# Finding a row's sources by segments of 128 columns, and a new order of the opening with four lists made early

## The chip, the cores and the metric

One core of a Trainium2 chip. The metric is the time of one execution on the device, in microseconds; the median of several executions is quoted with the lowest and the highest. All runs below are of the state "fast" but one: a run of 1221.58 us of "sums at +8" is marked slow and left out of its ratio. A profile is of one execution. Two profiles of the same kernel can differ by 8 us in a stage (349.2 and 341.1 us for steps 20 to 110 of the changed kernel), so a difference of a few microseconds between single profiles proves little; single steps that no wait disturbs repeat within a few tenths.

Names: PE is TensorE (matmul), PEld its weight load, DVE is VectorE, ACT is ScalarE, POOL is GpSimd, SP is SyncE, which here only issues DMAs. "Gate n" is the start of the DVE add that opens step n of the main loop; there are 320 steps.

## The reference

One layer of a graph network, batch B = 16, N = 1024 nodes, D = 256, float32:

```python
pre_u = einsum('bud,dk->buk', h, W1[:d]);  pre_v = einsum('bvd,dk->bvk', h, W1[d:])
hidden = relu(pre_u[:, :, None, :] + pre_v[:, None, :, :] + b1)
S   = sigmoid(einsum('buvk,ko->buvo', hidden, W2)[..., 0] + b2[0])
a_t = einsum('buv,bud->bvd', S * adj, h)
m_t = einsum('uv,bud->bvd', adj, h) * h
out = beta1 * h + beta2 * (a_t @ Wa + ba) + beta3 * (m_t @ Wm + bm)
```

`adj` is sparse: a row has its diagonal and a handful of other entries. The kernel works only on the entries that are not zero.

## The kernel before

Each of eight blocks of 128 rows needs a **list**: for every row the columns of its entries (at most S = 24), which are then dealt out to slots. The main loop takes 128 slots a step: fetch the source's row from a table in HBM (POOL, indirect), fetch the adjacency value, expand the destination's part (PE), add, relu and weigh (DVE), sigmoid (ACT), and aggregate (PE). Three lists are made before the loop and five between its steps. A list is a Python generator; each `yield` ends a part, and `script` (opening) and `advance` (loop) say when the next part of which list is emitted.

```python
def small(name):                       # PSUM: this pool has two buffers
    return psm.tile([P, 512], FP, name="misc")
def aside(vt):                         # where a list's matmul results go
    return psc.tile([P, GD], FP, name="pc") if vt < EARLY else small("pl")
NF = 5; EARLY = 3                      # buffers of fetched rows; lists made early
def clear(i):
    nc.gpsimd.memset(fetched[i][:, N if 1 <= i <= EARLY else 0:], 0.0)

def lists(vt):
    key = fetched[vt + 1][:, :N] if vt < EARLY else big.tile([P, N], FP, name="key", bufs=1)
    nc.gpsimd.dma_start(key, adjT[vt * P:(vt + 1) * P, :])
    yield
    ...                                # key = (adj != 0) * (N - column)
    nc.scalar.activation(unread, key, AF.Sign, accum_out=count)      # ACT counts the entries
    for s in range(0, S, 8):
        yield
        nc.vector.max(top[:, s:s + 8], key)                          # the 8 largest of 1024 columns
        if s + 8 < S:                                                # mask them, in place
            nc.vector.scalar_tensor_tensor(key, key, top[:, s + 7:s + 8], key, ALU.is_lt, ALU.mult)
    ...
    yield
    pw = aside(vt)                     # "sums": four small matmuls, PE -> PSUM
    for i in range(4):
        nc.tensor.matmul(pw[:, i:i + 1], sums[:, i]..., R[:, 0:1], start=True, stop=True)
    yield
    nc.vector.tensor_scalar(from_, pw[:, 1:2], base, low_, ALU.add, ALU.max)   # "from": DVE reads them
    ...                                # slots, four small writes of `whose` by ACT, sources

def rows(k):                           # one row block of a table: two half products
    tab = big.tile([P, GD], FP, name="tab")        # pool of two buffers
    ...

for i in range(EARLY, NT):
    for o in (0, 4, 5, 6, 7, 8, 9, 11, 13, 15, 17)[i == EARLY:]:
        advance[20 * (i - EARLY) + o] = (i,)
loads = dict(zip((0, 1, 2, 6, 9, 13, 17, 23), turn[NT:]))   # hT loads, each with a copy of x into
                                                            # the second table, issued by ACT
```

`misc` matters later. The same two PSUM buffers take, among others, the transposes of a finished half (`LT`), a swap (`X`), the halves of the second table (`tab`) and the sums of every list after the early ones. `hT` is x transposed, loaded in pieces of 512 KB for PE's products. `whose` tells which destination a slot belongs to; ACT writes it by four small DMAs for each list.

## Time and profile before

| | |
|---|---|
| time, 3 runs | 1238.86 us (1235.62 to 1244.02) |
| opening, to gate 0 | 89.2 us |
| steps 0 to 20 | 81.5 us |
| steps 20 to 110 | 352.4 us |
| step 110 to the end | 705.4 us |
| one list on DVE | 14.4 us |

The stages come from the starts of the DVE add. Read each one for itself: the opening waits on chains between engines, the steps up to 110 carry the lists and DVE limits them, and afterwards PE and the DMA engines are near their limit. The lines of the profile are shown in the prediction.

### The profile page before, as it was taken

What the parts mean: (1) busy time and instruction counts of PE and PEld (TensorE: products, weight loads), DVE (VectorE), ACT (ScalarE), POOL (GpSimd) and SP (SyncE); (2) the same over time, 40 slices, a digit from 0 to 9 for tenths busy, and PEclk for the clock granted to TensorE, in tenths of its full rate; (3) what the DMA queues carried; (4) which work ended last, traced back from release to release, by engine and by line L of the source; (5) the groups of instructions that cost most, each with busy time, mean ns of one, the idle gap of its engine ahead of it and who ended that gap; (6) DMA issues with size and microseconds to landing.
All of it is one profiled execution on the core that took longest, in us unless ns stands there. A gap on an engine that the chain in (4) does not pass through costs nothing. (4 is left out here: it accounts for less than half of the span.)

```text
span 1228.5 us, 23863 instructions
## 1 busy us (share of the span) xinstructions
PE 1108.6 (90%) x7697; PEld 723.5 (59%) x7697; DVE 1094.8 (89%) x3437; ACT 841.1 (68%) x2562; POOL 425.5 (35%) x419
## 2 busy tenths in 40 slices
PE   4767998997979989999999999999999999999996
PEld 3654665654546555666666556666666555665553
DVE  7659888999999899999899999889888999999994
ACT  1236675775656757777777777777777777777763
POOL 2227362362623614422333323222222333333330
PEclk8768999999999989999999999999999999999998
DMA  9569898898898989999999999999999988999992
GB/s 295 181 245 360 282 349 305 284 334 284 259 331 297 327 291 343 350 358 361 348 362 368 337 347 318 345 345 405 386 354 335 345 320 315 325 339 326 325 334 95
DMA packets 151975, 393.50 MB, mean 320 GB/s; under 512 B 16816, under 2 KB 110512, under 8 KB 115632
## 3 DMA queue, kind: packets, MB, share of 16 engines
q0 software_dynamic: 49792, 300.90, 66.4%
q1 hardware_dynamic: 85488, 76.03, 19.3%
q10 hardware_dynamic: 16560, 14.95, 3.7%
q8 instruction: 63, 1.03, 0.3%
q14 instruction: 72, 0.59, 0.1%
HBM read 395.88 MB, written 50.33 MB: 363 GB/s over the span
## 5 line engine op out<-in xcount | busy, mean ns | idle before, releaser
L452 POOL DMA_INDIRECT fetched<-table,uidx x320 | 329.9, 1031 | 705.0 <-PE acc L561 493.6
L544 DVE SCALAR_TENSOR_TENSOR t<-t,w_b 128x256 f32<-128x256 f32 x1280 | 469.9, 422 | 19.3 <-ACT X L412 0.5
L540 DVE TENSOR_TENSOR t<-fetched,pc 128x1024 f32<-128x1024 f32 x320 | 389.0, 1216 | 50.3 <-PE pc L524 25.2
L561 PE MATMUL acc<-fetched,left 128*32 128x256 f32 x4096 | 323.7, 392 | 26.9 <-ACT left L550 25.7
L550 ACT ACTIVATE left<-left,gt 128x32 f32<-128x32 f32 (+1 forms) x1280 | 299.4, 304 | 10.4
L524 PE MATMUL pc<-X,mark 128*128 128x512 f32 x640 | 247.3, 468 | 3.4 <-DVE t L540 1.9
L561 PEld LDWEIGHTS acc<-fetched,left 128*32 128x32 f32 x4096 | 122.7, 109 | 193.4 <-issue 68.0
L547 ACT ACTIVATE gt<-sc,b_b 128x4 f32<-128x4 f32 x320 | 95.4, 298 | 190.0 <-DVE t L544 189.5
L378 PE MATMUL misc<-w_u,hT 128*128 128x256 f32 x512 | 131.6, 406 | 23.5 <-ACT tab L394 12.9
L609 PE MATMUL misc<-w_m,LT 128*128 128x256 f32 x496 | 133.7, 392 | 0.0
L524 PEld LDWEIGHTS pc<-X,mark 128*128 128x128 f32 x640 | 118.4, 193 | 25.1 <-DVE LT L592 4.1
L609 PE MATMUL misc<-w_a,LT 128*128 128x256 f32 x496 | 127.3, 379 | 0.0
L378 PEld LDWEIGHTS misc<-w_u,hT 128*128 128x128 f32 x512 | 99.3, 202 | 45.1 <-ACT tab L394 14.4
L378 PE MATMUL misc<-w_v,hT 128*128 128x256 f32 x512 | 123.0, 384 | 0.0
L534 ACT ACTIVATE left<-onehot,val 128x128 f32<-128x128 bf16 (+1 forms) x320 | 116.6, 364 | 0.0
L609 PEld LDWEIGHTS misc<-w_m,LT 128*128 128x128 f32 x496 | 88.9, 189 | 34.8 <-issue 25.5
L336 POOL DMA_INDIRECT val<-in_adjT_dram,vidx x80 | 84.0, 1050 | 66.8 <-DVE b_p L194 40.0
L378 PEld LDWEIGHTS misc<-w_v,hT 128*128 128x128 f32 x512 | 98.5, 192 | 13.4
L544 DVE DVE_READ_ACCUMULATOR t<-t,w_b 128x1 f32 x1280 | 104.0, 81 | 0.0
L609 PEld LDWEIGHTS misc<-w_a,LT 128*128 128x128 f32 x496 | 94.2, 190 | 12.8
L569 ACT COPY ev<-acc 128x512 f32<-128x512 f32 x128 | 74.8, 585 | 28.9 <-PE acc L561 28.9
L424 ACT CAST X<-misc 64x512 fp32r<-64x512 f32 x128 | 74.3, 581 | 28.0 <-PE misc L421 23.9
(138 smaller groups left out, 860.1 us busy)
## 6 DMA issues: line engine op xcount, KB each, us to landing
hT<-in_xT_dram SPq DMA_DIRECT2D x40, 512.0 KB, 11.1
table<-tab SPq DMA_DIRECT2D x32, 512.0 KB, 5.2
h_blk<-in_x_dram SPq DMA_DIRECT2D x31, 512.0 KB, 13.4
out_dram<-h_blk SPq DMA_DIRECT2D x31, 512.0 KB, 5.5
table<-in_x_dram ACTq DMA_DIRECT2D x24, 512.0 KB, 11.8
fetched<-table,uidx POOLq DMA_INDIRECT x320, 7.9
table<-in_x_dram SPq DMA_DIRECT2D x8, 512.0 KB, 8.0
key<-in_adjT_dram POOLq DMA_DIRECT2D x5, 512.0 KB, 9.2
```

The source lines that it names most:

```text
L336: nc.gpsimd.indirect_dma_start(out=val[:, i, j:j + 1], out_offset=None, in_=adj_flat, in_offset=bass.IndirectOffsetOnAxis(ap=vidx[:, i, j: ...
L378: nc.tensor.matmul(p[:, bb * D:(bb + 1) * D], hT[:, 2 * h + bb, i, :], wt[:, i, :], start=(i == 0 and not begun), stop=(i == DC - 1), skip ...
L452: nc.gpsimd.indirect_dma_start(out=fetched[n % NF], out_offset=None, in_=table[g], in_offset=bass.IndirectOffsetOnAxis(ap=uidx[:, vt * NW ...
L524: nc.tensor.matmul(pcs[n][:, c], marks[n // TW][:, j * P:(j + 1) * P], cuts[k][:, w, c], start=True, stop=True)
L534: nc.scalar.activation(lefts[n][:, :m, :, 0, :], onehot[:, i, o:o + m, :].unsqueeze(2).to_broadcast([P, m, GB, V]), AF.Copy, scale=val[:, ...
L540: nc.vector.tensor_tensor(t, fetched[n % NF][:, :GD].rearrange("p (b d) -> p b d", b=GB), pcs.pop(n).rearrange("p (b d) -> p b d", b=GB), ...
L544: nc.vector.scalar_tensor_tensor(t[:, b, :], t[:, b, :], 0.0, w2_b, ALU.max, ALU.mult, accum_out=sc[:, b:b + 1])
L547: nc.scalar.activation(gt, sc, AF.Sigmoid, bias=b2_b)
L550: nc.scalar.activation(lefts[n][:, :m, b, 1, :], lefts[n][:, :m, b, 0, :], AF.Copy, scale=gt[:, b:b + 1])
L561: nc.tensor.matmul(accs[h][b * 2 * V:(b + 1) * 2 * V, r, :], left[:, i, b].rearrange("p k v -> p (k v)"), f[:, GD + b * D:GD + (b + 1) * D ...
L569: nc.scalar.copy(evs[q], accs.pop(q))
L609: nc.tensor.matmul(pz[:, bb * D:(bb + 1) * D], LTs[k][:, c, 2 * h + bb, i, :], wt[:, c, :], start=False, stop=(i == 1 and c == DC - 1), sk ...
```

## The change

The intent is to find the sources of a row with one pass over the keys, not five, and to rearrange the opening so that nothing in it waits for a buffer. DVE takes the 8 largest keys of each of eight segments of 128 columns; what lies below the largest eighth key of any segment is cut off, and the three passes run over the 64 candidates. Keys aren't overwritten. The early keys and the first group's table rows sit in the buffers of fetched rows, the memsets go, and four lists are made early.

```diff
-        return psc.tile([P, GD], FP, name="pc") if vt < EARLY else small("pl")
+        return psc.tile([P, GD], FP, name="pc") if vt < EARLY - 1 else small("pl")
-    EARLY = 3
+    EARLY = 4
-    def clear(i):
-        nc.gpsimd.memset(fetched[i][:, N if 1 <= i <= EARLY else 0:], 0.0)
-        nc.gpsimd.dma_start(key, adjT[vt * P:(vt + 1) * P, :])
+        (nc.sync if 2 <= vt < EARLY else nc.gpsimd).dma_start(key, adjT[vt * P:(vt + 1) * P, :])
+        yield
+        for c in range(N // P):
+            nc.vector.max(cand[:, c, :], key[:, c * P:(c + 1) * P])
+        yield
+        nc.vector.tensor_reduce(cut, cand[:, :, 7], AX.X, ALU.max)
+        nc.vector.scalar_tensor_tensor(keys, keys, cut, keys, ALU.is_ge, ALU.mult)
         for s in range(0, S, 8):
-            yield
-            nc.vector.max(top[:, s:s + 8], key)
+            nc.vector.max(top[:, s:s + 8], keys)
             if s + 8 < S:
-                nc.vector.scalar_tensor_tensor(key, key, ...)
+                nc.vector.scalar_tensor_tensor(keys, keys, ...)
-        tab = big.tile([P, GD], FP, name="tab")
+        tab = big.tile([P, GD], FP, name="tab") if tab is None else tab
+    tabs = [fetched[0][:, :GD], *(f[:, GD:] for f in fetched)]
     ...                                   (a new `script` for the opening)
-    for i in range(EARLY, NT):
-        for o in (0, 4, 5, 6, 7, 8, 9, 11, 13, 15, 17)[i == EARLY:]:
-            advance[20 * (i - EARLY) + o] = (i,)
+    advance = {0: (3,), 2: (3,), 4: (3,)}
+    for i, n in zip(range(EARLY, NT), (0, 30, 50, 80)):
+        for o in (0, 4, 5, 6, 7, 9, 11, 13, 15, 17):
+            advance[n + o] = (*advance.get(n + o, ()), i)
```

Two details of this diff are easily passed over. In the last lines, 8 is gone from the offsets: the sums are emitted at step +7 and read at +9, where they were emitted at +8. And the cut with all three passes is one part, where the search had been spread over three.

More of the change, by code (lines that the diff above doesn't have):

```diff
@@ L250, in lists @@
         nc.scalar.activation(unread, key, AF.Sign, accum_out=count)
+        yield
+        cand = wk.tile([P, N // P, 8], FP, name="cand", bufs=2)
+        for c in range(N // P):
+            nc.vector.max(cand[:, c, :], key[:, c * P:(c + 1) * P])
+        yield
+        cut = wk.tile([P, 1], FP, name="cut", bufs=2)
+        nc.vector.tensor_reduce(cut, cand[:, :, 7], AX.X, ALU.max)
+        keys = cand.rearrange("p c e -> p (c e)")
+        nc.vector.scalar_tensor_tensor(keys, keys, cut, keys, ALU.is_ge, ALU.mult)
         for s in range(0, S, 8):
-            yield
-            nc.vector.max(top[:, s:s + 8], key)
+            nc.vector.max(top[:, s:s + 8], keys)
             if s + 8 < S:
-                nc.vector.scalar_tensor_tensor(key, key, top[:, s + 7:s + 8], key, ALU.is_lt, ALU.mult)
+                nc.vector.scalar_tensor_tensor(keys, keys, top[:, s + 7:s + 8], keys, ALU.is_lt, ALU.mult)
         used = wk.tile([P, S], FP, name="used", bufs=4)
@@ L383, in add_row, with rows @@
                          start=True, stop=False, skip_group_check=True)
-    def rows(k):
+    def rows(k, tab=None):
         g, nt = k
-        tab = big.tile([P, GD], FP, name="tab")
+        tab = big.tile([P, GD], FP, name="tab") if tab is None else tab
         for h in range(2):
@@ L460 @@
     turn += [(1, vt) for _, vt in turn]
-    for i in range(2):
-        next(made[i])
+    tabs = [fetched[0][:, :GD], *(f[:, GD:] for f in fetched)]
     for i in range(NT):
+        if i < 2:
+            next(made[i])
         load_hT(turn[i])
-    for i in range(NF):
-        clear(i)
-    for i in range(2, EARLY + 1):
-        next(made[i])
+        if i in (5, 7):
+            next(made[i // 2])
     COPIES = 2
@@ L471 @@
         copy_h(turn[i], nc.sync)
-    script = ("r r 0 0", "r r 0", "r r 0 1", "0 r 1", "0 0 r r", "0 r 1", "r 0 0 v 1 r", "1 r 2 2", "1 1 r r h",
-              "1 r h 2", "1 1 h 2", "2 f h h", "2 2", "2", "2 2")
+    script = ("r 0 0", "r r 0", "r 1", "0 r 1 1", "0 0 r r", "1 r 0 2 2", "r 0 0 v 2", "1 1 r r 2",
+              "r 1 r 3 3", "1 1 2 2 r h", "2 r r h 3", "2 2 3 h", "3 3 f h h")
     m = 0
@@ L483 @@
                 if m % 2 == 0:
-                    piece = rows(turn[m // 2])
+                    piece = rows(turn[m // 2], tabs[m // 2] if m // 2 < len(tabs) else None)
                     next(piece)
@@ L655, in tail @@
         after(step + 1, add)
-    advance = {}
-    for i in range(EARLY, NT):
-        for o in (0, 4, 5, 6, 7, 8, 9, 11, 13, 15, 17)[i == EARLY:]:
-            advance[20 * (i - EARLY) + o] = (i,)
+    advance = {0: (3,), 2: (3,), 4: (3,)}
+    for i, n in zip(range(EARLY, NT), (0, 30, 50, 80)):
+        for o in (0, 4, 5, 6, 7, 9, 11, 13, 15, 17):
+            advance[n + o] = (*advance.get(n + o, ()), i)
     loads = dict(zip((0, 1, 2, 6, 9, 13, 17, 23), turn[NT:]))
```

## The prediction

> **What bounds the kernel now.** The page first: PE is busy 1108.6 of 1228.5 us (90%), DVE 1094.8 (89%), and the three DMA queues together take 89.4% of the sixteen engines. No engine is alone at the top, so averages decide nothing; I ask stage by stage. From the starts of the 320 gates (the DVE add of L540, one per step) the trace of the kernel before has three stages.
>
> - Opening: the first gate starts at 89.2 us. Until then only tables and lists are made.
> - Steps 0 to 110: from 89.2 to 523.1 us, 3.94 us a step. The lists 3 to 7 are made here, between gates.
> - Steps 110 to 320: from gate 110 at 523.1 to gate 310 at 1179.1 us, 3.28 us a step. No lists. The change adds and removes nothing here.
>
> The opening, in the timeline of all engines (columns: start, us, engine, line, operation; in brackets the idle time before and who ended it):
>
> ```profile
> 2.57 6.26 POOL L238 MEMSET fetched<- 128x2048 f32 x5
> 3.50 5.69 DVE L116 TENSOR_SCALAR upto<-ukey 128x640 f32<-128x640 f32 x1
> 12.85 1.21 DVE L249 SCALAR_TENSOR_TENSOR fetched<-fetched,ukey 128x1024 f32<-128x1024 f32 x1
> 14.09 1.23 DVE L253 MAX8 R<-fetched 128x8 f32<-128x1024 f32 x1
> 15.45 1.28 DVE L255 SCALAR_TENSOR_TENSOR fetched<-fetched,R 128x1024 f32<-128x1024 f32 x1
> ...
> 34.21 1.07 ACT L394 COPY tab<-misc 128x512 f32<-128x512 f32 x2 [17.54 <-DMA table<-tab]
> ...
> 36.37 1.28 DVE L255 SCALAR_TENSOR_TENSOR fetched<-fetched,R 128x1024 f32<-128x1024 f32 x1 [13.04 <-ACT unread L250]
> ...
> 74.94 1.00 POOL L452 DMA_INDIRECT fetched<-table,uidx  x1 [11.79 <-issue]
> ...
> 89.16 1.21 DVE L540 TENSOR_TENSOR t<-fetched,pc 128x1024 f32<-128x1024 f32 x1
> ```
>
> Three things to see. The DVE's 640-column scalar operation, which takes 0.55 us in the lists, takes 5.69 us beside the POOL memsets. ACT stands 17.5 us because the two tab buffers are still being written out; behind it in ACT's order is the count of list 1, and because the search overwrites the keys that ACT counts, DVE stands another 13.0 us. So one shortage of buffers stops PE, ACT and DVE together. The fetches begin only at 74.9, when the last table write has landed.
>
> The windows say the same (per engine busy us and instructions, granted PE clock, DMA share, GB/s):
>
> ```profile
> 20.00:40.00 20.00, 6.20 (x20) 5.13 (x21) 6.68 (x20) 2.71 (x5) 0.00 (x0) 0.58 1.06 298
> 40.00:60.00 20.00, 17.28 (x79) 14.39 (x78) 14.02 (x41) 5.49 (x10) 8.04 (x8) 0.91 0.44 147
> 60.00:80.00 20.00, 11.44 (x46) 9.49 (x46) 10.88 (x34) 5.07 (x9) 6.52 (x7) 0.77 0.44 134
> ```
>
> DMA is full to 40 us and under half used from 40 to 80: the opening is then bound by the chain through DVE, PE and ACT, not by bandwidth.
>
> For the second stage, windows of 40 us:
>
> ```profile
> 280.00:320.00 40.00, 33.86 (x232) 21.29 (x229) 38.57 (x129) 24.34 (x75) 11.17 (x11) 0.96 0.71 240
> 600.00:640.00 40.00, 39.54 (x290) 26.09 (x290) 37.50 (x119) 31.51 (x97) 12.47 (x13) 1.00 0.99 366
> ```
>
> At 280 DVE is busy 38.6 of 40 us and DMA only 0.71; at 600 PE and DMA are at their limit. So the list steps are DVE-bound and later ones are not. A check: steps 20 to 110 take 523.1 - 170.7 = 352.4 us, at 3.28 us a step they would take 295. The excess of 57 us is 14.3 for each of four lists, which is what one list costs DVE (14.4, below): there the lists come through in full.
>
> **The Trainium skill.** "SBUF — State Buffer", Who interferes with whom: GpSimd and a DVE operation of the two-port kind (tensor_scalar among them) share a port pair that is locked for a whole instruction. The trace agrees: 5.69 against 0.55 us, ending 0.4 us after the memsets. "VectorE: DVE Perf Modes", The TRN2 errata: a Vector operation costs (N+151)/0.96 ns, so short ones are mostly fixed cost, and the page advises 512 elements or more. MAX8 on 1024 columns should take 1224 ns, the trace has 1.22 to 1.23 us; I use it for the short ones, which this trace doesn't have (290 ns for 128 columns, 224 for 64, as estimates). The same page, Two Vector instructions with no wait between them: the next may start before the last has ended. In the trace, short ones without a wait start some 0.08 us before that end. "TensorE: Matmul & The Clock Gate", What's actually happening: an idle PE gets half the clock; the trace has 0.58 granted at 20 to 40 us.
>
> **The change part by part.**
>
> 1. Search of a row. Before: three MAX8 (3 x 1.23) and two maskings (2 x 1.28) over 1024 columns, each waiting for the last: 14.09 to 20.61, 6.5 us with the first wait; 6.3 without it. After: eight MAX8 of 128 columns without waits, 8 x (0.29 - 0.08) = 1.7; a reduction, a cut, three MAX8 and two maskings over 64 columns, seven dependent ones at about 0.25 = 1.75. Sum 3.4, so 2.9 saved. The rest of a list is unchanged: keys 1.2, bookkeeping 0.25, slots 4.0 (37.57 to 41.61), sources 2.6 (46.63 to 49.27). A list falls from 14.4 to 11.5 us of DVE. The inputs give at most 7 sources in any segment, so nothing spills into the slow remainder.
>
> 2. The keys aren't overwritten any more, so the 13.0 us wait for ACT's count goes.
>
> 3. Memsets gone: 6.3 us of POOL, and DVE's setup ends some 5 us sooner (7.7 instead of 12.85). Key 0 lands at 9.95, so list 0 starts at about 10: 2.9 gained.
>
> 4. Eight tab buffers instead of two for the first group: the 17.5 us wait goes.
>
> 5. The fourth list (number 3) moves ahead of the first gate, all but its last 2.6 us. Steps 20 to 110 now hold three lists, not four; steps 0 to 20 hold list 4 and the remainder of list 3, 14.1 against 14.4 us.
>
> 6. Keys 2 and 3 move to the SP queue. The bytes moved before the first fetch are the same, some 14.7 MB; at the 300 GB/s of the opening they need 49 us. That's a floor above which the new opening still ends, see next.
>
> **The new opening by hand**, along the order of each engine in the built program. DVE: list 0 searched by 15, list 1 by 20, slots of list 0 by 24, key 2 by 27. ACT gives the list-0 result only after the issue of four small copies (3.1 us before, at 43.06), which in the built program wait for the landing of earlier transfers, of which eight may be open, in a full queue: 30 to 34. Then sources of 0, rest of list 2, slots of 1, key 3: 43 to 46. Same round trip for list 1: sources of 1 by 49 to 52, slots of list 2 by 53 to 56. In the after order PE makes the last table row (two half rows) behind list 2's matmuls; add 4 to 5 us for it, ACT's copies behind the next issue, and the last table write goes out at 59 to 63 and lands 3.5 us later (70.55 to 73.91 before). First fetch at 63 to 67, against 74.9: 8 to 12 us gained. The gate also needs list 3's slots on DVE (69 to 72), ACT's four copies and mark (3 us), PE's expansion (2 us): gate 0 at 73 to 76, against 89.2: 13 to 16 gained. After that the fetches compete with the second table's transfers (DMA share 1.03 in 80 to 120), so the start of the fetches counts as much as that of the gate: I take **11 us**.
>
> **Main part.** Steps 20 to 110: DVE work falls by 4 x 14.4 - 3 x 11.5 = 23 us. PE is at 88% there (246 of 280 us in 200 to 480), and 246/(280 - 23) would be 96%, just what it holds at 600, so nearly all of it can come through: I take **20 us**. Steps 0 to 20: nothing.
>
> Sum: 31 us. 1238.9 - 31 = **1208 us**.
>
> **Rivals.** (a) DMA is the bound through the first 200 us, and an earlier start only moves the queue: the shares of 0.90 to 1.03 speak for it; against it, DVE waits for fetched rows in only 17.6 us in all after 80 us. Then the opening gives 5 and the sum is 25: 1214. (b) PE takes over when DVE is lighter in steps 20 to 110, as clock dips to 0.92 to 0.96 there hint; then the main part gives 10 and the time is 1218. (c) Everything before the first gate comes through, with PE warmer: 16 + 23 = 39 us, 1200. (d) The new order makes a fresh wait: ACT holds table copies behind the slots of a list, SP holds writes behind that; if list 2 comes 10 us later than I think, the opening gives nothing and the time is 1219. A longer time than before I can only see if the remainder loop ran, and the data exclude that.
>
> **Range and chances.** The rivals span 1200 to 1219, and the three runs of before scatter by 8 us: 1195 to 1223. The line of 2% is 1214, 6 us above my number, less than half of the way to the upper end: faster 0.68, within 2% 0.31, slower 0.01.
>
> **What will show it.** DVE's 640-column operation near 0.55 us; the eight MAX8 of a list near 0.29 us each and a search near 3.4; ACT without a wait for table writes and DVE without one for the count; first fetch at 63 to 67, first gate at 73 to 76; gate 110 less gate 20 at about 332 us; the steps after 110 unchanged at 3.28. I am wrong if the first gate is earlier but gate 20 isn't (a), if steps 20 to 110 keep 3.9 us while DVE has idle time (b), or if the short MAX8 cost much more than 0.3 us.

## The result, and the profile after

Four runs of each: 1227.09 us (1224.78 to 1227.23) after, 1239.64 (1235.62 to 1244.02) before. The ratio is 0.9894, 95% interval 0.9858 to 0.9930. A ratio is here always the mean time of one kernel's fast runs over that of the other's of the same rounds, so not quite the ratio of the medians quoted. So the change gains 1.1%, where I had said 2.5%; 1227 is above my upper end of 1223.

The opening after, in the timeline (columns as in the prediction):

```profile
3.49 0.49 DVE L116 TENSOR_SCALAR upto<-ukey 128x640 f32<-128x640 f32 x1
...
10.23 1.23 DVE L246 SCALAR_TENSOR_TENSOR fetched<-fetched,ukey 128x1024 f32<-128x1024 f32 x1 [2.51 <-DMA fetched<-in_adjT_dram]
...
11.49 1.65 DVE L253 MAX8 cand<-fetched 128x8 f32<-128x128 f32 x8
...
14.87 0.23 DVE L260 MAX8 R<-cand 128x8 f32<-128x64 f32 x1
...
32.77 0.18 DVE L317 TENSOR_TENSOR s_of<-slot_of,L 128x10 f32<-128x10 f32 x1 [5.35 <-ACT L L313]
...
68.62 1.00 POOL L459 DMA_INDIRECT fetched<-table,uidx  x1 [18.63 <-issue]
...
78.14 1.22 DVE L546 TENSOR_TENSOR t<-fetched,pc 128x1024 f32<-128x1024 f32 x1 [4.22 <-PE pc L530]
```

Against the lines of before: the 640-column operation takes 0.49 us, not 5.69. The eight MAX8 of 128 columns take 1.65 us together, and the search ends at 15.1, 3.6 us after its start, not 6.5. ACT's wait of 17.5 us and DVE's of 13.0 are gone; the longest that DVE is left with is 5.35 us for ACT's copy of list 0. First fetch at 68.6, gate 0 at 78.1.

Three windows that answer to those of before (same columns):

```profile
20.00:40.00 20.00, 14.24 (x69) 11.84 (x67) 13.61 (x64) 4.21 (x8) 3.16 (x3) 0.91 1.06 321
...
280.00:320.00 40.00, 35.00 (x236) 21.12 (x235) 35.83 (x115) 26.36 (x82) 21.93 (x22) 0.96 0.81 287
600.00:640.00 40.00, 38.91 (x287) 25.51 (x287) 36.98 (x117) 31.12 (x96) 11.85 (x13) 1.00 0.99 371
```

From 20 to 40 us PE has 14.24 us of work where it had 6.20, and at the same DMA share: the opening got denser as intended. At 280, DVE is busy 35.8 of 40 us, down from 38.6, though the two windows don't cover the same steps. Over the whole of steps 20 to 110 DVE is busy 306.2 us of 349.2 (306.1 of 341.1 in the second profile); before it was 327.4 of 352.5 (327.8 of 357.1). The work fell by 21 us, as intended, but DVE's idle time grew from 25 to 29 us before to 35 to 43 after. Something else holds those steps. The last window is as before.

Both kernels were profiled a second time (the first two experiments). The stages, with both profiles of each:

| stage | before | after | gained (means) | predicted |
|---|---|---|---|---|
| to gate 0 | 89.2, 90.4 | 78.1, 78.0 | 11.8 | 11 |
| steps 0 to 20 | 81.5, 82.2 | 96.9, 93.4 | **-13.3** | 0 |
| steps 20 to 110 | 352.4, 357.1 | 349.2, 341.1 | 9.6 | 20 |
| 110 to the end | 705.4, 706.0 | 700.9, 701.2 | 4.7 | 0 |

The opening's gain came, and 20 steps later it was gone. DVE has the same work in steps 0 to 20 as before (75.3 us before, 75.4 and 74.7 after), so what grew is its idle time. There are two stalls in these steps, both read here in the second profile of the changed kernel. The first, in steps 2 to 4, from its timeline:

```profile
84.40 0.66 ACTq L379 DMA_DIRECT2D table<-in_x_dram  x1
...
90.52 1.22 DVE L546 TENSOR_TENSOR t<-fetched,pc 128x1024 f32<-128x1024 f32 x1
...
95.27 0.58 ACTq L379 DMA_DIRECT2D table<-in_x_dram  x1
95.89 0.30 ACT L553 ACTIVATE gt<-sc,b_b 128x4 f32<-128x4 f32 x1 [8.59 <-DMA hT<-in_xT_dram]
...
96.60 2.55 PE L567 MATMUL acc<-fetched,left 128*32 128x256 f32 x16 [6.47 <-ACT left L556]
...
98.58 1.21 DVE L546 TENSOR_TENSOR t<-fetched,pc 128x1024 f32<-128x1024 f32 x1
```

ACTq is ACT issuing a DMA. It issues a copy of x into the second table at 84.40; the next it can issue only at 95.27. The sigmoid behind it in ACT's order, which needs nothing of the DMA, starts at 95.89 after 8.59 us put down to a load of hT. PE waits 6.47 us for the result. Gate 3 started at 90.52 and gate 4 comes at 98.58.

The second, in steps 7 to 10, from the same timeline:

```profile
112.31 1.05 PE L272 MATMUL misc<-R,sums 128*128 128x1 f32 x8
...
114.83 1.22 DVE L546 TENSOR_TENSOR t<-fetched,pc 128x1024 f32<-128x1024 f32 x1
...
116.25 0.56 ACT L588 COPY LT<-misc 128x512 f32<-128x512 f32 x1
...
116.87 1.11 PE L585 MATMUL misc<-ident,ev 128*128 128x128 f32 x4 [3.00 <-ACT LT L588]
...
118.65 0.80 PE L428 MATMUL misc<-low,swap 128*128 128x512 f32 x1 [0.67 <-ACT LT L588]
...
120.71 3.78 PE L385 MATMUL misc<-w_u,hT 128*128 128x256 f32 x8 [1.26 <-ACT X L431]
...
125.33 1.22 DVE L546 TENSOR_TENSOR t<-fetched,pc 128x1024 f32<-128x1024 f32 x1 [6.01 <-PE pc L530]
...
126.23 1.99 PE L385 MATMUL misc<-w_u,hT 128*128 128x256 f32 x8
...
128.03 0.26 DVE L277 TENSOR_SCALAR from<-misc,base,low__108 128x1 f32<-128x1 f32 x1
```

PE writes the sums of list 4 into a `misc` buffer at 112.31, and DVE reads them at 128.03. For these 16 us one of the two `misc` buffers is held, and everything else of PE's goes through the other one by turns: transpose, ACT copy, transpose (after 3.00 us), ACT copy, swap, ACT cast, half product. PE's granted clock was low there too: 0.50 from 116.0 to 124.5 us, and 1.00 again from 126.2. The eight matmuls of L385 take 3.78 us at 120.71 and 1.99 at 126.23. Gate 9, at 125.33, is 10.5 us after gate 8, at 114.83. In the kernel before the same step took 5.9 and 5.4 us, and there the sums were read 1.65 us after they were begun (first profile):

```profile
126.44 1.05 PE L265 MATMUL misc<-R,sums 128*128 128x1 f32 x8
...
128.09 0.27 DVE L270 TENSOR_SCALAR from<-misc,base,low__108 128x1 f32<-128x1 f32 x1
```

What these readings don't tell is which of the two costs how much, and whether a third thing (the loads that now overlap the first steps, the issue of fetches by POOL) would take the time back anyway. That's what the experiments are for.

### The profile page after: what moved, and what is told of

Its sections match the earlier page's. It is cut to its first block, busy times and chain, and to the rows that moved or that the text cites. A ratio compares the mean times of both kernels' runs of the same rounds, so it can differ in the third digit from the quotient of the medians.

```text
span 1225.1 us, 23939 instructions
## 1 busy us (share of the span) xinstructions
PE 1110.8 (91%) x7697; PEld 723.6 (59%) x7697; DVE 1068.5 (87%) x3517; ACT 844.0 (69%) x2562; POOL 416.3 (34%) x412
## 5 line engine op out<-in xcount | busy, mean ns | idle before, releaser
L556 ACT ACTIVATE left<-left,gt 128x32 f32<-128x32 f32 (+1 forms) x1280 | 300.3, 306 | 10.4
L530 PE MATMUL pc<-X,mark 128*128 128x512 f32 x640 | 249.8, 472 | 5.4 <-ACT mark L523 5.4
L553 ACT ACTIVATE gt<-sc,b_b 128x4 f32<-128x4 f32 x320 | 95.5, 299 | 158.8 <-DVE t L550 150.7
L385 PE MATMUL misc<-w_u,hT 128*128 128x256 f32 x512 | 132.7, 407 | 19.8 <-ACT fetched L401 8.4
L385 PEld LDWEIGHTS misc<-w_u,hT 128*128 128x128 f32 x512 | 99.3, 203 | 43.9 <-ACT fetched L401 8.9
L385 PE MATMUL misc<-w_v,hT 128*128 128x256 f32 x512 | 122.6, 383 | 0.0
L385 PEld LDWEIGHTS misc<-w_v,hT 128*128 128x128 f32 x512 | 98.3, 192 | 13.2
L575 ACT COPY ev<-acc 128x512 f32<-128x512 f32 x128 | 74.9, 585 | 41.6 <-PE acc L567 28.6
L585 PE MATMUL misc<-ident,ev 128*128 128x128 f32 x512 | 81.0, 289 | 15.8 <-DVE h_blk L619 8.5
```

The source lines that it names most:

```text
L385: nc.tensor.matmul(p[:, bb * D:(bb + 1) * D], hT[:, 2 * h + bb, i, :], wt[:, i, :], start=(i == 0 and not begun), stop=(i == DC - 1), skip ...
L530: nc.tensor.matmul(pcs[n][:, c], marks[n // TW][:, j * P:(j + 1) * P], cuts[k][:, w, c], start=True, stop=True)
L553: nc.scalar.activation(gt, sc, AF.Sigmoid, bias=b2_b)
L556: nc.scalar.activation(lefts[n][:, :m, b, 1, :], lefts[n][:, :m, b, 0, :], AF.Copy, scale=gt[:, b:b + 1])
L585: nc.tensor.transpose(pt[:, i * P:(i + 1) * P], ev[:, r, c * P:(c + 1) * P], ident)
```

## The experiments

Sixteen kernels were run in four jobs. Each job had its own chip and its own runs of the kernel before, so ratios of different jobs are compared by their intervals.

| run | ratio to before | 95% interval |
|---|---|---|
| before again | 1.0018 | 1.0000 to 1.0035 |
| after again | 0.9896 | 0.9863 to 0.9929 |
| segments only | 0.9790 | 0.9761 to 0.9820 |
| opening only | 1.0103 | 1.0076 to 1.0129 |
| copies on SP | 0.9899 | 0.9863 to 0.9935 |
| list 4 later | 0.9936 | 0.9912 to 0.9959 |
| three lists | 0.9907 | 0.9872 to 0.9942 |
| more DVE work | 1.0001 | 0.9980 to 1.0022 |
| sums at +8 | 0.9812 | 0.9759 to 0.9865 |
| three lists, sums at +8 | 0.9826 | 0.9774 to 0.9879 |
| segments only, sums at +7 | 0.9961 | 0.9944 to 0.9978 |
| three lists, values early | 0.9808 | 0.9766 to 0.9849 |
| sums at +8, copies later | 0.9789 | 0.9738 to 0.9840 |
| the same, split | 0.9753 | 0.9701 to 0.9806 |
| three lists, split, copies later | 0.9762 | 0.9707 to 0.9817 |
| segments only again | 0.9786 | 0.9736 to 0.9836 |

### The two kernels again

No edit.

> The kernel before, unchanged, timed against itself: a null test, and a second trace. Its runs so far lie between 1235.6 and 1244.0 us, but the profiled one took 1230.3. If that trace was a lucky one, the new one should be longer by several us, with the difference in steps 20 to 110 (352 us in the first trace). If it was typical, the new one should have 352 us there again, within 2 us. The ratio should be 1.00 within 0.004.

> The changed kernel, unchanged, for a second trace (the first has no landings of DMAs) and more timings: ratio 0.989 within 0.004. First gate near 78 us, gate 10 near 131 us again if the loss of the 11 us between the two is systematic; if it was chance, gate 10 near 120 to 125 us.

Measured: 1233.97 us (1229.59 to 1240.09) and 1216.76 (1215.51 to 1222.15). Both agree with the first comparison, and their profiles are the second ones of the table above. The loss is systematic: gate 10 came at 129.9 us again (131.3 in the first profile).

### The parts of the change alone

Segments only, on the kernel before, its opening, three early lists and offsets kept:

```diff
+            nc.vector.max(cand[:, c, :], key[:, c * P:(c + 1) * P])      # eight of them
+        yield
+        ... cut ...
+        yield
         for s in range(0, S, 8):
-            yield
-            nc.vector.max(top[:, s:s + 8], key)
+            nc.vector.max(top[:, s:s + 8], keys)
```

> The kernel before with the segment search alone (same opening, same steps of a list). DVE does some 2.8 us less in each list, 14 us in the five lists of the main part and some 3 to 8 us more in the opening, where the wait for the count goes. Theory A (my prediction: DVE bounds the steps in which lists are made): at least 12 us faster, ratio 0.990 or less. Theory B (DVE has slack there; PE, ACT and DMA waits set the pace): under 4 us faster, ratio 0.997 to 1.0, with more DVE idle time and the same step time.

Measured: 1207.10 us (1201.01 to 1214.66), ratio 0.979. Gate 0 at 83.1, steps 0 to 20 in 76.0, steps 20 to 110 in 343.7; a second profile, of the last job, has 82.0, 80.2 and 346.5. One part of the change gains twice what the whole does.

Opening only: the changed kernel with the old search in place of the segments, its five passes in two parts. The keys are overwritten again.

> The changed kernel with the old search (three MAX8 and two maskings over 1024 columns) in its lists: the new opening and the fourth list alone. Theory A: the first gate comes at about 82 to 86 us instead of 78, and the search costs 4 lists x 2.9 = 12 us in the main part, so some 12 to 18 us slower than the changed kernel, ratio near 1.0. Theory B: what the opening gains is lost again by gate 10 to 20 in any case, and DVE has slack later: time within 4 us of the changed kernel, ratio 0.988 to 0.993.

Measured: 1243.95 us (1241.13 to 1246.77), slower than before. First fetch at 84.9, gate 0 at 95.5. With five passes of 1024 columns for each of four lists, and DVE still waiting for ACT's count (7.4 and 6.9 us), the new order is late, later than the 82 to 86 us that I expected. The two parts add up: 2.1% gained and 1.0% lost are the 1.05% of the whole. So the segments are good and the new order costs 13 us, although with the segments it brings gate 0 forward (78 us, against 82 and 83 with segments only).

### First attempts at the loss

Copies on SP: every copy of x into the second table is issued by SP, not ACT.

```diff
-                copy_h(loads[n])
+                copy_h(loads[n], nc.sync)
```

> The changed kernel with the copies of x into the second table (steps below 30) issued by SP instead of ACT. In the traces ACT stands 8.6 us at step 2 to 3, because it may issue the second such copy only when a table load (hT) eight transfers earlier has landed, and the gates behind it wait. Theory H (ACT's issue order is what eats the earlier start): steps 0 to 20 fall from 93 to 97 us to about 85, and the kernel is 6 to 12 us faster than the changed one (ratio to before 0.980 to 0.985). Theory D (the DMA engines are full there, and the loads themselves are what the steps wait for): the wait moves to PE or DVE, steps 0 to 20 stay at 92 to 97 us, ratio 0.987 to 0.992.

Measured: 1218.53 us (1213.94 to 1222.36), ratio 0.9899, no gain. The wait had moved: now ACT stood 12.5 us at its four small `whose` writes for list 3, again put down to a load of hT. This says that the engine isn't the point. In the built program each DMA waits for the transfer that last used its one of eight places, and an hT load still in flight holds up whoever draws its place next. The semaphores in the packed trace show it: in the second profile of the changed kernel the copy issued at 95.27 waits on the same semaphore, number 112, as the hT load issued at 69.35, and this load landed at 95.25.

List 4 later: the lists of the loop at steps 20, 40, 60, 80.

```diff
-    for i, n in zip(range(EARLY, NT), (0, 30, 50, 80)):
+    for i, n in zip(range(EARLY, NT), (20, 40, 60, 80)):
```

> The changed kernel with list 4 made in steps 20 to 37 instead of 0 to 17 (then 40, 60, 80). If list 4's DVE work in the crowded first steps is the cause, steps 0 to 20 fall by its 11.5 us to about 84, and steps 20 to 110 rise by as much: total unchanged within 3 us, unless the first steps are where it hurts more. If transfers and ACT's issue order are the cause, steps 0 to 20 stay above 90 us, steps 20 to 110 rise by 8 to 11 us, and the kernel is 4 to 10 us slower than the changed one.

Measured: 1222.32 us (1217.96 to 1232.73), ratio 0.9936. Steps 0 to 20 fell to 83.4 us, but steps 20 to 30 took 47.2 where the changed kernel took 37.7; step 28 to 29 alone took 10.4 us, not 4.8. The stall went along with the list.

Three lists: the new opening with three lists early, the loop's lists at 0, 20, 40, 60, 80, sums at +7.

```diff
-    EARLY = 4
+    EARLY = 3
-    ... "r 1 r 3 3", "1 1 2 2 r h", "2 r r h 3", "2 2 3 h", "3 3 f h h")
+    ... "1 r 1 r", "1 1 2 2 r h", "2 r r h", "2 2 h", "f h h")
-    advance = {0: (3,), 2: (3,), 4: (3,)}
-    ... zip(range(EARLY, NT), (0, 30, 50, 80))
+    ... 20 * (i - EARLY)
```

> The changed kernel with three lists made ahead instead of four, and list 3 made in steps 0 to 17 as before: new search, new buffers, no memsets, but not the fourth list. If the fourth list (its small copies on ACT and its rest in steps 0 to 4, list 4 moved into steps 0 to 17) is what costs, it should beat the segments alone: first gate at 72 to 76 us, steps 0 to 20 near 77 us, ratio 0.972 to 0.979. If any earlier start is swallowed, because the loads of the second table land at 91 to 95 us whatever comes before, the gates 3 to 10 come at the same times as in the segments alone (gate 10 at 117 to 120 us): ratio 0.978 to 0.982.

Measured: 1219.68 us (1216.68 to 1226.70), ratio 0.9907. That lies outside the ranges of both my theories, which ended at 0.982. Gates 0 to 8 take 28.3 us, against 36.8 in the changed kernel: without the remainder of a fourth list in steps 0 to 4, the first copies draw places that small loads of biases had used (semaphores 114 to 116), and no wait of ACT for hT is left. But step 8 to 9 takes 10.6 us again, and steps 20 to 30 take 48.1. The second stall doesn't need the fourth list.

More DVE work: three needless MAX8 of 1024 columns in each list of the loop.

```diff
+        if vt >= EARLY:
+            for c in range(3):
+                nc.vector.max(junk[:, c, :], key)
```

> The changed kernel with three unused MAX8 over 1024 columns (3 x 1.22 us) added to each of the lists 4 to 7: 14.6 us more DVE work, of which 11 us in steps 20 to 110 and 3.7 in steps 0 to 20. Theory A (DVE on the path where lists are made): 10 to 15 us slower than the changed kernel, ratio to before 0.997 to 1.002. Theory B (slack on DVE): under 4 us slower, ratio 0.989 to 0.993.

Measured: 1232.09 us (1225.71 to 1235.87), ratio 1.0001. The twelve take 13.8 us of DVE, and the time grows by about 13 us. In the steps that make lists, extra DVE work is paid nearly in full, so the lighter search should count there too. That leaves waits as what takes the gain back, and the next runs test one of them.

### The held buffer, forwards and backwards

Forwards, one number of the changed kernel altered:

```diff
-        for o in (0, 4, 5, 6, 7, 9, 11, 13, 15, 17):
+        for o in (0, 4, 5, 6, 8, 9, 11, 13, 15, 17):
```

> The changed kernel with one number altered: the sums of a list (the matmul into one of the two small PSUM buffers) are made at step +8 instead of +7, one step before VectorE reads them at +9, for the fourth and later lists. Theory (held buffer): in the changed kernel that buffer is held from about 112.5 to 128.5 us, 16 us, and step 8 to 9 takes 10.5 to 13 us; here it is held about 3 us, step 8 to 9 takes 3.5 to 6 us, gates 0 to 20 take 84 to 89 us (93 to 97 in the changed kernel), and the kernel is 6 to 12 us faster than the changed one: ratio to the kernel before 0.980 to 0.985. Rival (the loads of the opening, which now overlap the first steps, take the time back wherever the sums are made): step 8 to 9 stays at 10 us or more, ratio 0.988 to 0.992.

Measured: 1212.15 us (1203.02 to 1221.58, the slow run included), ratio 0.9812 from the four fast runs. From its timeline:

```profile
111.94 1.09 PE L585 MATMUL misc<-ident,ev 128*128 128x128 f32 x8
...
122.73 1.05 PE L272 MATMUL misc<-R,sums 128*128 128x1 f32 x8
...
124.41 0.27 DVE L277 TENSOR_SCALAR from<-misc,base,low__108 128x1 f32<-128x1 f32 x1
```

Both transposes run in one go (eight matmuls at 111.94), for the sums aren't made before 122.73 and are read 1.7 us later. The kernel is some 10 us faster than the changed kernel, by the two ratios to before, as the theory said; the two intervals just touch. Step 8 to 9 falls only to 7.2 us, short of what I expected, and steps 0 to 20 take 89.3.

Backwards, on the kernel with the segments alone: the `yield` ahead of the passes is left out for the late lists, and so is offset 8, so that the sums come at +7.

```diff
+        if vt < EARLY:
             yield                                  # between the cut and the passes
-        for o in (0, 4, 5, 6, 7, 8, 9, 11, 13, 15, 17)[i == EARLY:]:
+        for o in (0, 4, 5, 6, 7, 9, 11, 13, 15, 17)[i == EARLY:]:
```

> The reverse test: the kernel before with the segment search alone (ratio 0.979), with the sums of the later lists moved from +8 to +7, as in the changed kernel. Theory (held buffer): the small PSUM buffer is held for over 10 us and stalls of 6 to 10 us appear at steps 8 to 9 and 28 to 29; ratio 0.987 to 0.994. Rival (the step of the sums does not matter): ratio 0.977 to 0.981, steps 8 to 9 at 3.5 to 5 us.

Measured: 1225.61 us (1221.72 to 1230.85), ratio 0.9961, some 20 us slower than segments alone and worse than the 0.994 at the end of my range. From its timeline, lines of DVE and PE:

```profile
107.73 1.05 PE L277 MATMUL misc<-R,sums 128*128 128x1 f32 x8
...
110.42 1.22 DVE L552 TENSOR_TENSOR t<-fetched,pc 128x1024 f32<-128x1024 f32 x1
...
120.18 1.22 DVE L552 TENSOR_TENSOR t<-fetched,pc 128x1024 f32<-128x1024 f32 x1 [5.25 <-PE pc L536]
...
122.87 0.27 DVE L282 TENSOR_SCALAR from<-misc,base,low__108 128x1 f32<-128x1 f32 x1
```

Written at 107.73, read at 122.87, and between the two gates of 110.42 and 120.18 DVE waits 5.25 us for PE's expansion. That step takes 9.8 us, against 3.5 and 3.8 in the two profiles of segments alone; step 28 to 29 takes 9.3, against 3.3 in both. The same stall appears in a kernel that has none of the new opening. That this edit also joins two parts of the list, as the changed kernel does, is a second difference; how much of the 20 us that is, the split below lets one judge.

### Three lists, mended halfway

The three-lists kernel with the one number altered:

```diff
-        for o in (0, 4, 5, 6, 7, 9, 11, 13, 15, 17)[i == EARLY:]:
+        for o in (0, 4, 5, 6, 8, 9, 11, 13, 15, 17)[i == EARLY:]:
```

> The opening of the changed kernel with three lists made early instead of four, and the sums at +8. Theory (held buffer): gate 0 stays near 77 us, gates 0 to 20 take 76 to 79 us (83.7 with three lists and sums at +7), steps 20 to 30 about 40 us (48.2 there, with a wait of VectorE of 5.75 us on a PSUM buffer), ratio 0.970 to 0.977, faster than segments alone (0.979) by the earlier start. Rival (loads swallow the earlier start): the time gained at gate 0 is lost by gate 10 and the ratio is 0.978 to 0.982. If the held buffer is not the cause: 0.988 to 0.992 as with three lists before.

Measured: 1208.79 us (1204.45 to 1218.53), ratio 0.9826, short of my expectation. Gate 0 at 75.4, steps 0 to 20 in 80.5, steps 20 to 30 in 41.6. Step 8 to 9 still takes 7.2 us, and here is why, in its timeline:

```profile
98.29 0.16 DVE L256 TENSOR_REDUCE cut<-cand 128x1 f32<-128x8 f32 x1
...
100.48 1.21 DVE L546 TENSOR_TENSOR t<-fetched,pc 128x1024 f32<-128x1024 f32 x1
...
103.33 0.30 ACT L553 ACTIVATE gt<-sc,b_b 128x4 f32<-128x4 f32 x1 [2.73 <-DVE t L550]
...
104.81 1.04 ACT L588 COPY LT<-misc 128x512 f32<-128x512 f32 x2
...
105.42 0.80 PE L428 MATMUL misc<-low,swap 128*128 128x512 f32 x1 [3.60 <-ACT LT L588]
...
110.58 1.22 DVE L546 TENSOR_TENSOR t<-fetched,pc 128x1024 f32<-128x1024 f32 x1 [3.74 <-PE pc L530]
```

The cut and the three passes fill DVE from 98.29 to 100.48 ahead of gate 7, so ACT gets its sums late (2.73 us idle before 103.33), copies the transposes behind that, and PE waits 3.60 us for the copies. PE then works at a granted clock of 0.50 (105.4 to 110.6 us).

The same with the values of list 1 fetched in the opening, where POOL is idle:

```diff
-              ... "2 r r h", "2 2 h", "f h h")
+              ... "2 r r h w", "2 2 h", "f h h")
+            elif c == "w":
+                fetch_val(T)
```

> As the three lists with sums at +8, with the two fetches of values of the first groups of list 1 issued by GpSimd in the opening, where it is idle, not in steps 1 to 5. In the kernel before GpSimd issues one row fetch and two value fetches a step at 1.3 us each there, 3.9 us a step. If that issue bounds the first steps, they come 3 to 8 us sooner than without it and the ratio falls by 0.003 to 0.006 below that of its sibling; if the loads or VectorE bound them, within 2 us of its sibling.

Measured: 1209.97 us (1205.45 to 1210.91), ratio 0.9808, the same as its sibling. POOL's issue doesn't bound the first steps.

### What was still open

Copies later, on the changed kernel with sums at +8. The hT loads stay where they are.

```diff
-            if loads[n] not in begun or n < 30:
+            if loads[n] not in begun:
                 copy_h(loads[n])
+        if n in copies:
+            copy_h(copies[n])
+    copies = dict(zip((8, 10, 12, 14, 16, 20, 24, 28), turn[NT:]))
```

> The changed kernel with the sums at +8, and the copies of x into the second table issued from step 8 on instead of at steps 0, 1, 2 and so on. In its sibling with the sums at +8 alone, ScalarE may not issue the second and third of these copies before the loads of hT issued at 68.9 and 69.7 us have landed at 94.9 and 99.3 us, and its gate work waits 8.7 and 2.4 us behind them in order; gates 0 to 8 took 37.0 us. Theory (in-order issue): without the copies there ScalarE does not wait, gates 0 to 8 take 28 to 31 us as with three lists (28.0), and the kernel is 5 to 9 us faster than its sibling: ratio 0.973 to 0.978. Rival (the data of the loads are what the first steps wait for, and the copies only show it): gates 0 to 8 stay at 34 us or more and the ratio stays at 0.980 to 0.983.

Measured: 1208.36 us (1201.80 to 1209.31), ratio 0.9789. Step 3 to 4 falls from 8.2 to 3.3 us, and no wait of ACT for hT is left in steps 0 to 10. Gates 0 to 8 take 32.4 us, not 37.0. I had expected 28 to 31; list 3's last parts are DVE work that stays here, which I take for the rest. The loads aren't what these steps waited for: left alone, the two in question landed at 98.2 and 105.5 us in this profile, and gate 4 started at 97.8. Nor did they gain by the copies' absence: 25.7 and 32.2 us from issue to landing, against 26.0 and 29.7 in the sibling. Its ratio is a little above my range, and its interval overlaps the sibling's, so the gain of this edit is seen in the steps and not in the times. In the profiled run the first fetch went out at 71.8, some 4 us later than in its siblings with the same opening, which I take for scatter.

Split: the cut and the three passes are two parts again for the late lists.

```diff
+        if vt >= EARLY:
+            yield
         for s in range(0, S, 8):
...
-        for o in (0, 4, 5, 6, 8, 9, 11, 13, 15, 17):
+        for o in (0, 4, 5, 6, 7, 8, 9, 11, 13, 15, 17):
```

> As the last, and the cut and the three passes over the 64 candidates are two parts in steps 6 and 7, as in the kernel before, not one in step 6. With three lists the one part made gate 8 wait and ScalarE's copies after it, and step 8 to 9 took 7.2 us; with segments alone, where the parts are two, 3.5 us. Theory: step 8 to 9 takes 3.5 to 5 us and, over four lists, the kernel is 3 to 10 us faster than its sibling: ratio 0.966 to 0.974. Rival (the part of 2.2 us is paid once either way): within 2 us of its sibling.

Measured: 1201.10 us (1194.48 to 1205.53), ratio 0.9753. Its timeline:

```profile
108.97 1.21 DVE L548 TENSOR_TENSOR t<-fetched,pc 128x1024 f32<-128x1024 f32 x1
...
110.00 1.99 PE L387 MATMUL misc<-w_u,hT 128*128 128x256 f32 x8
...
112.49 1.22 DVE L548 TENSOR_TENSOR t<-fetched,pc 128x1024 f32<-128x1024 f32 x1
...
113.38 1.05 PE L274 MATMUL misc<-R,sums 128*128 128x1 f32 x8
...
115.18 0.27 DVE L279 TENSOR_SCALAR from<-misc,base,low__108 128x1 f32<-128x1 f32 x1
```

Gate 9 comes 3.5 us after gate 8, the eight half-product matmuls take 1.99 us (3.78 in the changed kernel), and the sums are read 1.8 us after they were begun. Steps 0 to 20 take 79.9 us and steps 20 to 110 take 333.1. The ratio is just above my range of 0.966 to 0.974. On the same chip the median is 7.3 us below the sibling's. The profile is of the fastest of the five runs (1194.48 us), so its stages flatter this kernel.

Three lists with all three mends (on the three-lists kernel with sums at +8, the diffs of the last two experiments), and segments alone beside them on the same chip, with no edit to its first run:

> Three lists early, sums at +8, two parts, copies later. If all that was lost is the held buffer, the one part and the copies, this keeps the 7 us of the opening over segments alone: ratio 0.971 to 0.975, against 0.979 for segments alone on the same chip. If something else takes the time back, the same as segments alone within 2 us. Between this and the last stands what the fourth early list is worth.

> Segments alone once more, beside the others on the same chip: ratio 0.976 to 0.982 as before. Needed because the kernels to compare are within 1% of it.

Measured: 1203.46 us (1198.68 to 1208.81), ratio 0.9762, and 1206.78 (1202.75 to 1212.22), ratio 0.9786. The last agrees with 0.979 of its first run; the first is just above the 0.971 to 0.975 that I expected. With five runs each and intervals of half a per cent to either side, the three best kernels can't be put in order. Nor do their profiles do it: gate 110 starts at 490.6 with four lists, 500.5 with three, 508.7 with segments alone, but the profiled runs were the fastest, the median and the slowest of their five. The mended changed kernel is clearly better than the kernel before and than the changed kernel as it was (0.9701 to 0.9806, against 0.9863 to 0.9929); whether it gains more than 2% is not settled by that interval.

## Why the prediction was wrong, and where it was right

**Right: the opening, step by step.** The 640-column operation takes 0.49 us with the memsets gone, against 5.69 beside them, which agrees with the shared port of GpSimd and VectorE (the Trainium skill, "SBUF — State Buffer", Who interferes with whom). The first search takes 3.6 us where I said 3.4. The waits for table buffers and for ACT's count are gone. Gate 0 comes 11.8 us sooner, against 11. It starts at 78, a little later than my 73 to 76, and the first fetch at 68.6, later than my 63 to 67. So both gains fell short of their ranges (7 us of 8 to 12 for the fetch, 12 of 13 to 16 for the gate), and that my 11 held is partly luck.

**Right: the rest after step 110, in what the change does to it.** The 4.7 us gained there have no cause that I know. The two runs of segments alone took 710.0 and 701.7 us for the same stretch, so I call it scatter.

**Wrong: "Steps 0 to 20: nothing."** They lost 13.3 us, which is more than the opening brought. I had compared sums of DVE work for these steps, 14.1 against 14.4 us. The sums were right (DVE is busy some 75 us there before and after), but I took equal work for equal time, and no sum of work shows a wait. DVE's idle time in these steps grew from 6.2 and 7.1 us to 21.5 and 18.7. Three things of the order were in the diff:

| mend, one after the other | steps 0 to 20 | step 3 to 4 | step 8 to 9 | steps 20 to 110 |
|---|---|---|---|---|
| the changed kernel, 2nd profile | 93.4 | 8.1 | 10.5 | 341.1 |
| sums at +8 | 89.3 | 8.2 | 7.2 | 337.7 |
| and copies later | 84.7 | 3.3 | 6.7 | 339.8 |
| and cut and passes split | 79.9 | 3.2 | 3.5 | 333.1 |

The held `misc` buffer, ACT's in-order wait at a DMA that it may not issue yet, and the joined part of a list cost 4.1, 4.6 and 4.8 us in single profiles of two chips. Such a difference by itself is within the scatter of this stage (96.9 and 93.4 in the two profiles of the changed kernel, 76.0 and 80.2 in those of segments alone); the single steps are the firmer evidence, and each mend shortens the step that it should. With all three mended the steps take 79.9 us, against 81.5 and 82.2 before, and DVE idles 5.5 us: then my "nothing" holds. The in-order wait is long because the earlier gate 0 brings ACT to the copies while the hT loads are still on their way: the first, issued at 69.35 us, landed at 95.25. With segments alone it landed at 91.1 and ACT came to the same copy at 91.1. The wait isn't new in kind: at the third copy the second profile of the kernel before has one of 4.0 us, and that of segments alone one of 6.5. The new order makes it longer, and in the first profile of the changed kernel the longest wait (6.7 us) fell on the third copy, in step 5 to 6, not in step 3 to 4. Rival (d) named the class, a fresh wait made by the new order, but looked for it in the opening. Rival (a) said that gate 0 would be earlier and gate 20 not, which is what happened, but gave the wrong cause: with the hT loads untouched, moving the copies and the sums and splitting the joined part gives the time back.

**Wrong in size: 20 us in steps 20 to 110.** The work was sized rightly: a list keeps DVE busy 2.9 us less (14.3 us before, 11.3 after; 2.3 less if overlapping instructions are counted twice), the fourth list leaves these steps, and DVE's busy time in them fell by 21 us, against my 23. The needless MAX8 count nearly one for one. But only 9.6 us of the time came, because DVE's idle time grew by about as much as the rest. The failed step is "nearly all of it can come through". Part of what held it back is the same held buffer, at each of the lists at 30, 50 and 80: steps 38, 58 and 88 took 4.9 to 5.4 us in both profiles of the changed kernel, and 3.3 in every profile of it with the sums at +8, some 5 us in all. (The stall is 10 us only at steps 8 and 28, where the second table's rows need `misc` as well.) The joined part is the likely rest. With all mends DVE idles 28.0 us and the stage takes 333.1 us, against my 332, but in the profile of the fastest run; the kernel's median is 6.6 us longer. Rival (b), PE as the next bound, is not what stopped the gain, since the mended kernel does the same PE work and PE is busy 93% there.

**The sum.** As written the change ended within 2% of the kernel before, to which I had given 0.31. Mended, the kernel gains 2.5% of 1234 us, some 30 us (24 to 37 by the interval), which is what I had predicted for the change as it stood. My estimate was one of the work, and the change as written didn't let the work run.

**Open.** How the 20 us of the reverse test divide between the held buffer and the joined part was not measured by itself. The forward tests suggest some 10 us for the buffer (0.9896 to 0.9812 with four lists, 0.9907 to 0.9826 with three) and 4 to 7 for the joined part. A third `misc` buffer was not tried. Nor is it settled whether the fourth early list is worth its place, as the timed runs don't separate it from three.

## What to carry to other kernels

When a change moves the point at which something is emitted, follow each buffer from its writer to its reader in the new order: one of two PSUM buffers held across two steps turned a pipeline into a relay. Look at each engine that issues DMAs and also computes: here ACT stood 8.6 us at a DMA whose place wasn't free yet, with its sigmoid behind it, and starting earlier made that wait longer. And try the parts of a change alone early: here half of it was worth twice the whole.

## What the Trainium skill lacked or had wrong

- "VectorE: DVE Perf Modes", The TRN2 errata, advises operations of 512 elements or more. Taken as a rule it would have spoken against the segments: eight MAX8 of 128 columns and seven operations on the 64 candidates took 3.6 us, five passes over 1024 columns took 6.5. Its formula holds for one of them alone (0.28 us on average, 290 ns by the formula); eight without waits took 1.65 us, about 0.2 each, because each starts before the last has ended, as the prediction said with the same page. The page measured the formula on an addition; that it fits MAX8 (1.23 us on 1024 columns, 1224 ns by the formula) is what these runs add.
- "Perfetto Trace Analysis", Optimization Strategy, says that a gap that repeats can mean too few buffers for the next tile. It lacks the case seen here: two buffers were enough, but one of them was held 16 us because its reader is emitted two steps after its writer. One step later for the writer took the kernel from 0.9896 to 0.9812 of the time before.
- "DMA: Bandwidth & Descriptors", Issuing engines are not separate DMA queues, says that choosing several issuing engines saves only the time to initiate, usually small. In these runs an issue on ACT that waited for an earlier transfer's place held ACT's other work for 8.6 us, and moving the copies to SP moved the wait (12.5 us) to another of ACT's DMAs. The section doesn't speak of it.
